# Moving VectorE and POOL instructions in the opening steps of a two-layer graph-attention kernel, and one block transpose in every later step

## Chip, cores and metric

One core of one Trainium2 chip. The metric is the device time of one execution in microseconds (us); the kernel before has a median of 3182.92 us over three executions (3182.58 to 3184.44). Engines are named as in the profile: PE is TensorE, DVE is VectorE, ACT is ScalarE, POOL is GpSimd, SP is SyncE.

## The reference, cut to what matters

64 graphs of 256 nodes with 512 features go through two layers of masked attention. Layer 0 has 4 heads of 64, layer 1 has 8.

```python
h = relu(layernorm(x));  x = x + L0(h, adj)      # layer 0
h = relu(layernorm(x));  x = x + L1(h, adj)      # layer 1
# L0:  q, k, v = h@Wq, h@Wk, h@Wv                (4 heads)
#      attn = softmax(where(adj, q k^T / 8, -max));  out = (attn v) @ Wo + bo
# L1:  h = layernorm(h)*gamma + beta;  q, k, v = split(h @ w_qkv^T)   (8 heads)
#      attn = softmax(where(adj | eye, q k^T / 8, -1e9)); out = (attn v) @ w_out^T + b_out
```

## The kernel before, in words

**Tiling.** The 64 graphs are done two at a time, so there are 32 steps (`s` = 0 to 31); a step's tokens are 512, in four row tiles of 128. Projections are done with seven products of half-size blocks in place of eight (`PRODUCT`, line 402). A **set** is those seven products of one matrix, on PE one after the other in the order 1, 6, 5, 2, 7, 3, 4 (`SET`). The sums of activations that products need are made by `act_sums0` and `act_sums1` on POOL (lines 412 to 417), the sums of weights by `weight_sum` (line 409).

**Banks.** Every product goes to one of four PSUM banks, taken in rotation by `mm_tile`. Products 1, 5 and 7 hold their bank, because 2, 3 and 4 accumulate in it later (`SHARED`). After a product a drain instruction has to read the bank: products 1 and 2 on ACT (lines 750 and 758), the others as an addition on DVE (lines 752 to 762, in the order 6, 5, 7, 3, 4). So product 3 can't begin before product 5 is drained, nor product 4 before product 7 is, and a later matmul that comes round to the same bank waits in the same way. Output projections (`combine`) drain the same way at lines 769 to 780.

**Softmax.** The pipeline calls attention work a **visit**: `scores` (PE, line 933), `mask_scores` (DVE, 956), `exponentials` (ACT, 961). The sums over keys go another way: `key_halves` adds the two key halves on POOL into the single buffer `pd` (968), `turn_keys` transposes `pd` in 32x32 blocks on DVE (974), `key_quarters` reduces that on DVE (981), and one visit later `key_sums` ends it on PE (1032), inverts it on DVE (1036) and sends it through DRAM to all partitions (`line`, 1043, then `oT<-line`, 1047). `weigh_out` multiplies by v (PE, 1004) and copies out on ACT (1016), `normalise` multiplies by the inverse on POOL (1063). A visit of layer 1, and of layer 0 after the first step, has two head pairs, i = 0 and 1; the first layer-0 step takes its two head pairs in visits of their own.

**Norms and transposes.** `norm0` makes the moments on DVE (589, 590) and, at the fourth tile, the scales on POOL; `scale_row` applies them on ACT (605). From step 2 on, the transpose of h in layer 0 goes by `turn_blocks` on DVE (699), `move_blocks`, 16 DMAs of SP (711), and `place_h` on ACT. `neighbours` (DVE, 524) finds rows with an edge and `neighbours_out` and `neighbours_in` send that through DRAM. `first_bias` (511) and `second_bias` (651) add the output biases to the residual tile `xt` on POOL; `load_graph` (505) loads `xt` from ACT's queue.

**What orders the work.** All of it is written out by hand: `at(period, place, fn, ...)` puts a call at time `6.4*period + place` (6.2 for negative periods), the list is sorted by that number, and the calls are made in that order (`for _, _, fn, args in sorted(events...)`). PE, DVE, ACT and POOL take their instructions strictly in that order (`manual_schedule` at line 359 names these four engines; SP is not among them). An engine that waits therefore holds back everything that comes later in its list. Within a period, step s has layer 1's first q/k set at 0, the output projection of the step before at 1, visit X at 2 (`AT_X`) with the v set of layer 1 from 2 to 3, layer 0's output projection of the next step at 3, layer 1's second q/k set at 3.5, the next visit at 4.5 (`AT_Q0`), and so on. Before step 0's period lie two opening periods, in which the weights are also transposed by PE (`weight_block`, 469, copied out at 474).

Of the kernel before, what the change touches and what calls it, by code (L numbers as in the profile page):

```python
# [315 lines left out]
def fast_path(  # L316
# [19 lines left out]
    nc = tc.nc  # L336
# [89 lines left out]
    wo1 = const.tile([P, NB, HP1, HD], FP, name="wo1")  # L426
# [261 lines left out]
    def by_tensor(s, lyr):  # L688

        return s == 0 or s == (1, NSTEP - 1)[lyr]  # L690
# [382 lines left out]
    def at(period, place, fn, *args):  # L1073
        events.append((period * (PERIOD if period >= 0 else FIRST) + place, len(events), fn, args))
# [15 lines left out]
    def visit(period, w, prev, cur):  # L1090

        w -= 0.0003
        s, lyr, prs = prev
        last = (s, lyr) == (NSTEP - 1, 1)
        if prs:
            if prs[0] == 0 and not last:
                at(period, w - 0.0002, place_values, s, lyr)
            at(period, w - 0.0001, key_sums, s, lyr, prs)
            for i, pr in enumerate(prs):
                if not last:  # L1100
                    at(period, w, weigh_out, s, lyr, pr)
                    at(period, w + (0.55 if len(prs) == 1 else (0.3, 0.75)[i]), normalise, s, lyr, pr)
        z, q = w > AT_Z - 0.01 and period < NSTEP - 2, abs(w - AT_Q0) < 0.01 and 0 <= period < NSTEP - 2
        for i, pr in enumerate(cur[2]):
            unit = (*cur[:2], pr)
            one = cur[:2] == (0, 0)
            at(period, w, scores, *unit, i == 1)
            at(period, w, mask_scores, *unit, 0)
            at(period, w + 1 / 7 if one else w, mask_scores, *unit, 1)
            for g, place in enumerate((0.05, 0.22) if one else ((0.02, 0.03), (0.15, 0.3))[i]):  # L1110
                at(period, w + place, exponentials, *unit, g)
            for e, place in enumerate((0.23, 0.3) if one else ((0.1, 0.11), (0.495, 0.496) if z else (0.435, 0.436) if q else (0.35, 0.36))[i]):
                at(period, w + place, key_halves, *unit, e)
            if cur[:2] == (1, 0):
                turn, add, key = 0.112, 0.113, (*cur[:2], (0, 1), pr)
            else:
                turn, add = (
                    (0.31, 0.311) if one else ((0.49, 0.491), (0.63, 0.92))[i] if z else
                    ((0.43, 0.431), (1.02, 1.021))[i] if q else ((0.29, 0.291), (0.6, 0.72))[i]
                )  # L1120
                key = (*cur, i)
            at(period, w + turn, turn_keys, cur[0])
            at(period, w + add, key_quarters, *key)

    AT_X, AT_C0, AT_QK, AT_Q0, AT_V0, AT_H1, AT_Z = 2.0, 3.0, 3.5, 4.5, 5.5, 6.06, 6.2
    LAST_QK = 4.0
    none, L0, L1A, L1B = (NSTEP, 0, ()), (0, 1), (0, 2), (1, 3)
    for s in range(NSTEP - 1):
        visit(s, AT_X, (s + 1, 0, L0), (s, 1, L1A))
        if s < NSTEP - 2:  # L1130
            visit(s, AT_Q0, (s, 1, L1A), (s, 1, L1B))
            visit(s, AT_Z, (s, 1, L1B), (s + 2, 0, L0))

    p = NSTEP - 2
# [15 lines left out]
    for s in range(NSTEP):  # L1150

        p = s - 2
# [5 lines left out]
        for t in range(NT):  # L1158
            at(p, (0.5 + 0.4 * t, 1.95 + 0.1395 * t)[s] if s < 2 else (0.95, 1.05, 1.2, 1.35)[t], norm0, s, t)
            if s == 0:  # L1160
                at(p, 0.95 + 0.4 * t, first_scale, t)
            else:
                at(p, 1.6 + 0.001 * t if s != 1 else 2.6 + 0.1 * t, scale_row, s, t)
            if not by_tensor(s, 0):
                at(p, AT_X - 0.00035 + 0.00001 * t, turn_blocks, s, 0, t)
        if not by_tensor(s, 0):
            at(p, AT_X - 0.00031, move_blocks, s)
        for g in range(G):
            at(p, (1.8, 2.7)[s] if s < 2 else 0.94 + 0.001 * g, neighbours, s, g)
        if s < 2:  # L1170
            at(p, (2.9, 2.72)[s], neighbours_rows, s)
            at(p, (FIRST_Q0 + 0.285, 3.59)[s], neighbours_turn, s)
        else:
            at(p, 0.945, neighbours_out, s)
            at(p, 1.9, neighbours_in, s)
        at(p, (FIRST_Q0 + 0.1425, 3.583)[s] if s < 2 else 2.5, adjacency_turn, s)
        at(p, (FIRST_Q0 + 0.3, 3.74)[s] if s < 2 else 3.1, mask0, s)
# [13 lines left out]
        for t in range(NT):  # L1191
            place = (FIRST_V0 + 0.14 * t - (0 if t else 0.0005), (4.31, 5.02, 5.16, 5.31)[t])[s] if s < 2 else AT_V0 + 0.14 * t
            at_dense(p, place, 0.14, project_v0, s, t)
        p = s - 1
        if s == 0:
            p -= 2.23 / FIRST
        edge = 0 if s == 0 else 1 if s == NSTEP - 1 else 2
        if edge < 2:
            at(p, (0.0, 0.2)[edge], load_x, s)
        else:  # L1200
            at(p, AT_X + 0.005, load_graph, s, 1)
            at(p, AT_X + 0.025, load_graph, s, 0)
        for k, t in enumerate(NORM1):
            at(p, (1.55, 1.5, (2.34, 2.5, 2.85, 2.86)[k])[edge], first_bias, s, t)
        if edge == 2:
# [9 lines left out]
        for k in range(NT):  # L1215
            at(p, ((2.901, 3.041, 3.181, 3.321), (2.99919, 2.99933, 2.99947, 2.99961), (3.79, 3.8, 3.94, 3.95))[edge][k], norm1, s, k)
            at(
                p, ((3.042, 3.182, 3.322, 3.323), (2.99948, 3.2, 3.3, 3.45), (4.08, 4.22, 4.23, 4.37))[edge][k],
                norm1_rest, s, k,
            )  # L1220
            at(p, (10.9 + 0.1 * k, 6.5 + 0.1 * k, 5.6 + 0.01 * k)[edge], second_bias, s, k)
            place = ((3.6112, 3.6113, 3.7502, 3.7503)[k], 3.6 + 0.01 * k, AT_Q0 - 0.0002 + 0.00001 * k)[edge]
            at(p, place, scale_row, s, NORM1[k])
            if edge == 2:
                at(p, AT_Q0 + (0.15, 0.16, 0.29, 0.3)[k], turn_blocks, s, 1, NORM1[k])
# [3 lines left out]
        turn = (3.763, 3.9995, AT_H1)[edge]  # L1229
# [4 lines left out]
        p = s  # L1234
        if s < NSTEP - 1:
# [3 lines left out]
            p, place = (s + 1, 1.0) if s < NSTEP - 2 else (s, LAST_QK + 2)  # L1239
# [5 lines left out]
        else:  # L1245
            p = s - 1
# [22 lines left out]
    for i in range(16):  # L1269

        place = (
            *(3.3 - 3.93 + (1 + k) / 7 - 0.0005 for k in range(7)), 0.5205,
            *(0.53 + 0.14 * (k + 1) - 0.0005 for k in range(4)), *(FIRST + 0.9995 for k in range(4)),
        )[i]
        at(-1, place, lambda i=i: weight_block(blocks[i // 4], i // 4, i % 4))
    for i in range(4):
        at(-1, 0.1 + 0.01 * i, weight_sum, nc.vector, wqkv1[:, :, :, 0, :], i)
        at(-1, 0.54 + 0.0001 * i, weight_sum, nc.gpsimd, wqkv1[:, :, :, 1, :], i)
        at(0, 0.3, weight_sum, nc.gpsimd, wqkv1[:, :, :, 2, :], i)
        at(0, 2.8 + 0.3 * i, weight_sum, nc.gpsimd, wo1, i)  # L1280
    for _, _, fn, args in sorted(events, key=lambda e: e[:2]):
        fn(*args)

# [1 line left out]
def kernel(tc, *args):  # L1285
    nc = tc.nc
    B, N, _ = args[0].shape
    P = 128
    with tc.tile_pool(name="guard", bufs=1) as guard:
        extremes = guard.tile([P, B // 2 * 3 + 4], FP, name="extremes")  # L1290
        ident = guard.tile([P, P], FP, name="ident")
        make_identity(nc, ident)
        fast_path(tc, *args, ident, extremes)
        safe = guard.tile([1, 1], I32, name="safe")
        with tc.tile_pool(name="gps", bufs=1, space=bass.MemoryType.PSUM) as ps:
            top = guard.tile([P, 1], FP, name="top")
            nc.vector.tensor_reduce(top, extremes, axis=mybir.AxisListType.X, op=ALU.max)
            row = ps.tile([1, P], FP, name="row")
            nc.tensor.transpose(row, top, ident)
            all_top = guard.tile([1, 1], FP, name="all_top")  # L1300
            nc.vector.tensor_reduce(all_top, row, axis=mybir.AxisListType.X, op=ALU.max)
            nc.vector.tensor_scalar(safe, all_top, LIMIT, None, op0=ALU.is_le)
        flag = nc.values_load(safe[0:1, 0:1], min_val=0, max_val=1, skip_runtime_bounds_check_because="a comparison gives 0 or 1")
        with tc.If(flag < 1):
            general_path(tc, *args)
# [29 lines left out]
```

## Time and profile before

| | before |
|---|---|
| median of three executions | 3182.92 us |
| the profiled execution, its own time | 3188.26 us |
| its span | 3186.3 us |
| PE busy | 3143.5 us, 99% |
| POOL busy | 2240.4 us, 70% |
| DVE busy | 2147.2 us, 67% |
| ACT busy | 1248.1 us, 39% |
| DMA engines, mean rate | 75 GB/s |
| granted PE clock, mean | 0.997 |

The profiled execution took 5.3 us more than the median; sums made from its rows are made against its own time. In the page, a row gives a line of the code, an engine, an operation, the count, busy time, the mean time of one in ns, and the idle time of that engine just before such instructions with what ended it. In a timeline, the first number is the start in us from the beginning of the span, the second the duration, and a bracket at the end is idle time before the piece and its releaser.

### The profile page before, as it was taken

To read this page: it belongs to the slowest core of one execution; us is meant where nothing else is said; L and a number is where in the kernel's file an instruction comes from. 1 tells how busy PE (TensorE), PEld (TensorE's weight loads), DVE (VectorE), ACT (ScalarE), POOL (GpSimd) and SP (SyncE) were. 2 spreads that over 40 slices of the span, in tenths; PEclk is the share of its full clock that TensorE was granted. 3 is DMA by queue.
4 is the path that set the end of the run, shared out by engine and by line. 5 is a ranking of instruction groups with operands and counts; after the bars stand their busy time and mean duration, and the time that the engine had idled before them with its cause. 6 is when DMAs were issued, how large, how long until landed. Compare 5 with 4: busy or idle time off the path is not lost.

```text
span 3186.3 us, 54549 instructions
## 1 busy us (share of the span) xinstructions
PE 3143.5 (99%) x20660; PEld 2584.4 (81%) x20660; DVE 2147.2 (67%) x3590; ACT 1248.1 (39%) x2226; POOL 2240.4 (70%) x2124
## 2 busy tenths in 40 slices
PE   8899999999999999999999999999999999999999
PEld 6688888888888888888888888888888888888887
DVE  6576676666766766766666666667666666666666
ACT  4343433444343434334343434343343434343431
POOL 6667767777667677677776676776777766767753
PEclk9999999999999999999999999999999999999999
DMA  3221322312223223223222232232231222322301
GB/s 125 65 81 53 90 64 80 90 54 81 72 79 85 81 54 90 65 80 92 56 77 72 79 85 76 59 90 64 81 92 56 76 72 79 85 69 64 91 28 48
DMA packets 179851, 237.42 MB, mean 75 GB/s; under 512 B 65272, under 2 KB 69504, under 8 KB 179584
## 3 DMA queue, kind: packets, MB, share of 16 engines
q1 hardware_dynamic: 162832, 202.02, 22.7%
q10 hardware_dynamic: 16752, 31.86, 3.2%
q8 instruction: 165, 2.70, 0.4%
q14 instruction: 102, 0.84, 0.1%
HBM read 136.45 MB, written 34.40 MB: 54 GB/s over the span
## 4 chain that ended last, share of the span: by engine, by line
PE 87%; POOL 6%; DMA 4%; DVE 1%; issue 1%; ACT 0%; SPq 0%; ACTq 0%; POOLq 0%; DVEq 0%
PE mm L816 36%; PE mm L873 16%; PE sc L1004 9%; PE mm L857 7%; PE sc L933 7%; PE mm L843 7%; PE mm L933 2%; DMA out_dram<-xt 2%; POOL xt L511 2%; POOL pd L968 2%; DMA xt<-in_x_dram 1%; POOL oT L1063 1%; PE mm L1032 1%; POOL xt L784 0%; PE mm L899 0%
## 5 line engine op out<-in xcount | busy, mean ns | idle before, releaser
L816 PE MATMUL mm<-hT,wqkv 128*128 128x256 f32 x3584 | 790.0, 381 | 5.4 <-DVE qk L754 5.4
L816 PEld LDWEIGHTS mm<-hT,wqkv 128*128 128x128 f32 x3584 | 679.0, 190 | 109.4 <-issue 11.8
L968 POOL TENSOR_TENSOR pd<-p 128x512 f32<-128x512 f32 x383 | 480.2, 1276 | 404.4 <-ACT p L961 266.5
L873 PE MATMUL mm<-wo,oT 128*128 128x256 f32 x2632 | 587.4, 381 | 7.4 <-POOL oT L415 5.2
L873 PEld LDWEIGHTS mm<-wo,oT 128*128 128x128 f32 x2632 | 498.5, 190 | 86.5 <-POOL n L573 8.0
L956 DVE TENSOR_TENSOR p<-sc,n 128x512 f32<-128x512 f32 x579 | 362.7, 681 | 266.8 <-PE sc L933 265.4
L961 ACT ACTIVATE p<-p 128x512 f32<-128x512 f32 x766 | 431.1, 623 | 135.7 <-DVE p L956 134.6
L857 PE MATMUL mm<-wqkv,hT 128*128 128x256 f32 x1792 | 404.9, 383 | 6.9 <-DVE v L756 6.8
L816 PE MATMUL mm<-hT,wqk 128*128 128x256 f32 x1792 | 400.3, 383 | 1.2 <-DVE qk L756 1.0
L857 PEld LDWEIGHTS mm<-wqkv,hT 128*128 128x128 f32 x1792 | 334.4, 190 | 64.5 <-DVE v L756 11.6
L816 PEld LDWEIGHTS mm<-hT,wqk 128*128 128x128 f32 x1792 | 339.0, 191 | 57.3 <-issue 11.7
L1004 PE MATMUL sc<-p,v 128*32 128x256 f32 x6128 | 351.5, 380 | 0.0
L784 POOL TENSOR_TENSOR xt<-xt,u 128x512 f32<-128x512 f32 x183 | 230.1, 1272 | 98.8 <-DVE xt L773 71.3
L933 PE MATMUL sc<-qk 64*128 64x256 f32 x2320 | 295.1, 386 | 3.4 <-ACT oT L1016 3.4
L974 DVE STREAM_TRANSPOSE turned_p<-pd 128x1024 f32<-128x1024 f32 x192 | 237.5, 1237 | 83.2 <-POOL pd L968 82.8
L1004 PEld LDWEIGHTS sc<-p,v 128*32 128x32 f32 x6128 | 190.2, 110 | 118.4 <-issue 0.3
L933 PEld LDWEIGHTS sc<-qk 64*128 64x128 f32 x2320 | 219.9, 187 | 62.9 <-issue 39.2
L1063 POOL TENSOR_TENSOR oT<-oT 128x512 f32<-128x512 f32 x188 | 240.3, 1278 | 4.9 <-DMA oT<-line 4.9
L605 ACT ACTIVATE h<-h,mr,r 128x512 f32<-128x512 f32 x252 | 184.8, 804 | 141.6 <-POOL mr L601 137.7
L981 DVE TENSOR_REDUCE part<-turned_p 128x32 f32<-128x1024 f32 x192 | 232.8, 1213 | 4.4
L843 PE MATMUL mm<-wv,hT 128*128 128x256 f32 x1024 | 227.0, 379 | 0.0
L843 PEld LDWEIGHTS mm<-wv,hT 128*128 128x128 f32 x1024 | 194.2, 190 | 26.8 <-issue 0.3
(141 smaller groups left out, 3743.2 us busy)
## 6 DMA issues: line engine op xcount, KB each, us to landing
h<-blocks SPq DMA_DIRECT2D x960, 64.0 KB, 2.0
oT<-line SPq DMA_DIRECT2D x376, 128.0 KB, 3.9
h<-in_x_dram SPq DMA_DIRECT2D x31, 1024.0 KB, 5.8
out_dram<-xt SPq DMA_DIRECT2D x62, 512.0 KB, 4.0
xt<-in_x_dram ACTq DMA_DIRECT2D x60, 512.0 KB, 6.6
ne<-row SPq DMA_DIRECT2D x30, 256.0 KB, 4.9
ad<-in_adj_dram SPq DMA_DIRECT2D x32, 128.0 KB, 8.9
wr<-in_L_gnn_w_qkv_dram SPq DMA_DIRECT2D x3, 1024.0 KB, 8.8
```

What stands on the lines that cost most here:

```text
L816: nc.tensor.matmul(bank[:, k, :], w[:, wa, c, k, a * P:(a + 1) * P], st["hT"][:, ba, c, :], start=first and (k, c) == (0, 0), stop=(k, c) ...
L843: nc.tensor.matmul(bank, st["hT"][:, b0 + t // NIC * step, c % HC, i:i + P], wv0[:, c, :], start=(c == 0), stop=(c == NC - 1),)
L857: nc.tensor.matmul(bank[:, t, :], st["hT"][:, ba, c, t * P:(t + 1) * P], wqkv1[:, wa, c, 2, :], start=first and (t, c) == (0, 0), stop=(t, ...
L873: nc.tensor.matmul(bank[:, t, :], oT[:, ba, c, t * P:(t + 1) * P], w[:, wa, c, :], start=first and (t, c) == (0, 0), stop=(t, c) == (NIC - ...
L933: nc.tensor.matmul(sc[g][e][:, kc, :], qk[rows, 1, k0:k0 + P], qk[rows, 0, g * N:(g + 1) * N], start=True, stop=True,)
L956: nc.vector.tensor_tensor(p[e][:, g], sc[e], neg[:, :, g, :], ALU.add)
L961: nc.scalar.activation(p[e][:, g], p[e][:, g], AF.Exp, scale=SCALE)
L968: nc.gpsimd.tensor_tensor(st["pd"][:, e], p[e][:, :, 0, :], p[e][:, :, 1, :], ALU.add)
L974: nc.vector.transpose(st["turned_p"], st.pop("pd").rearrange("p e g (b k) -> p (e g b) k", k=32))
L981: nc.vector.tensor_reduce(st["part", lyr, prs][:, i], st.pop("turned_p"), axis=mybir.AxisListType.X, op=ALU.add)
L1004: nc.tensor.matmul(po[r0:r0 + 32, g, :], st[f"v{lyr}"][:, g * NIC + kc, pr * P + r0:pr * P + r0 + 32], p[r0 // DH][:, g, kc, :], start=(kc ...
L1063: nc.gpsimd.tensor_tensor(dst, dst, invb, ALU.mult)
```

## The change

Only numbers in the hand-written order change, and with them the order of calls. No instruction is added or taken away.

- First layer-0 set, second head pair: `turn_keys` and `key_quarters` go from 0.31 to 0.53 of their visit, behind the copy of the first transposed weight block.
- Layer-0 visits of step 1: `turn_keys` and `key_quarters` of both head pairs, and `key_halves` of the second, go out of the opening into layer 1's first q/k set of step 0.
- Step 2: `neighbours` and `neighbours_out` go from 0.94 to 0.6; `scale_row` from 1.6 to 2.35; `turn_blocks` from just before visit X to 2.9 to 2.99, `move_blocks` to 3.0.
- Step 0: `second_bias` goes from 2.47 to 2.77 up to 0.95; the four weight sums of `wo1` go from 2.8 to 3.7 up to 1.1.
- Step 1: `load_graph` goes from 2.005 and 2.025 to 1.2.
- Visit X of every step (and the last visits): `turn_keys` of head pair i = 1 goes from 0.6 to 0.715, behind the drain of product 7 of v (0.7133); its `key_quarters` goes from 0.72 to 1.001 in visit X, behind the drain of product 4, and to 0.87 in the last visits.

```diff
             for e, place in enumerate((0.23, 0.3) if one else ((0.1, 0.11), (0.495, 0.496) if z else (0.435, 0.436) if q else (0.35, 0.36))[i]):
-                at(period, w + place, key_halves, *unit, e)
+                if unit == (1, 0, 1):
+                    at(0, 0.45 + place, key_halves, *unit, e)
+                else:
+                    at(period, w + place, key_halves, *unit, e)
             if cur[:2] == (1, 0):
-                turn, add, key = 0.112, 0.113, (*cur[:2], (0, 1), pr)
+                period, w, key = 0, 0.0, (*cur[:2], (0, 1), pr)
+                turn, add = ((0.44, 0.441), (0.715, 0.87))[pr]
             else:
                 turn, add = (
-                    (0.31, 0.311) if one else ((0.49, 0.491), (0.63, 0.92))[i] if z else
-                    ((0.43, 0.431), (1.02, 1.021))[i] if q else ((0.29, 0.291), (0.6, 0.72))[i]
+                    ((0.31, 0.311), (0.53, 0.531))[pr] if one else ((0.49, 0.491), (0.63, 0.92))[i] if z else
+                    ((0.43, 0.431), (1.02, 1.021))[i] if q else ((0.29, 0.291), (0.715, 1.001 if w < AT_X else 0.87))[i]
                 )
...
-                at(p, 1.6 + 0.001 * t if s != 1 else 2.6 + 0.1 * t, scale_row, s, t)
+                at(p, (2.6 + 0.1 * t, 2.35 + 0.001 * t)[s - 1] if s < 3 else 1.6 + 0.001 * t, scale_row, s, t)
             if not by_tensor(s, 0):
-                at(p, AT_X - 0.00035 + 0.00001 * t, turn_blocks, s, 0, t)
+                at(p, AT_X - 0.00035 + 0.00001 * t if s > 2 else 2.9 + 0.03 * t, turn_blocks, s, 0, t)
         if not by_tensor(s, 0):
-            at(p, AT_X - 0.00031, move_blocks, s)
+            at(p, AT_X - 0.00031 if s > 2 else 3.0, move_blocks, s)
         for g in range(G):
-            at(p, (1.8, 2.7)[s] if s < 2 else 0.94 + 0.001 * g, neighbours, s, g)
+            at(p, (1.8, 2.7)[s] if s < 2 else (0.6 if s == 2 else 0.94) + 0.001 * g, neighbours, s, g)
...
-            at(p, 0.945, neighbours_out, s)
+            at(p, 0.61 if s == 2 else 0.945, neighbours_out, s)
...
-            at(p, AT_X + 0.005, load_graph, s, 1)
-            at(p, AT_X + 0.025, load_graph, s, 0)
+            at(p, AT_X + 0.005 if s > 1 else 1.2, load_graph, s, 1)
+            at(p, AT_X + 0.025 if s > 1 else 1.2, load_graph, s, 0)
...
-            at(p, (10.9 + 0.1 * k, 6.5 + 0.1 * k, 5.6 + 0.01 * k)[edge], second_bias, s, k)
+            at(p, (9.38 + 0.001 * k, 6.5 + 0.1 * k, 5.6 + 0.01 * k)[edge], second_bias, s, k)
...
-        at(0, 2.8 + 0.3 * i, weight_sum, nc.gpsimd, wo1, i)
+        at(0, 1.1, weight_sum, nc.gpsimd, wo1, i)
```

## The prediction, made before the result was known

> **What bounds the kernel now.** I read the share of busy time first, then busy time by stretches of 100 us, then PE's own waits, then the timelines of PE, DVE and POOL around each wait. The stretches, with PE's busy time first, show where PE is not full.
>
> ```profile
> 0.00:100.00 100.00, 85.67 (x485) 66.63 (x485) 60.60 (x112) 44.25 (x88) 67.22 (x78) 0.98 0.38 120
> 100.00:200.00 100.00, 85.88 (x566) 68.16 (x567) 60.79 (x105) 36.36 (x67) 72.07 (x71) 0.93 0.22 61
> 200.00:300.00 100.00, 98.21 (x648) 80.91 (x647) 67.25 (x113) 39.58 (x71) 70.80 (x68) 1.00 0.27 75
> 900.00:1000.00 100.00, 99.99 (x657) 82.76 (x656) 68.59 (x116) 38.89 (x69) 71.30 (x68) 1.00 0.27 74
> ```
>
> PE is the bound: 99.99 of 100 us in the middle. What order alone can win lies in the first 160 us, with a few us later. PE's timeline names the places; the bracket is the idle time before the piece and what ended it.
>
> ```profile
> 52.44 0.66 PE L469 MATMUL mm<-ident,wr 128*128 128x128 f32 x4 [4.39 <-ACT wqkv L474]
> 103.99 5.61 PE L816 MATMUL mm<-hT,wqkv 128*128 128x256 f32 x16 [5.38 <-DVE qk L754]
> 120.23 1.40 PE L933 MATMUL sc<-qk 64*128 64x256 f32 x7 [3.41 <-ACT oT L1016]
> 137.50 1.99 PE L857 MATMUL mm<-wqkv,hT 128*128 128x256 f32 x8 [1.19 <-DVE v L756]
> 145.58 4.65 PE L873 MATMUL mm<-wo,oT 128*128 128x256 f32 x13 [5.22 <-POOL oT L415]
> 439.56 1.99 PE L857 MATMUL mm<-wqkv,hT 128*128 128x256 f32 x8 [0.58 <-DVE v L756]
> 446.90 1.10 PE L873 MATMUL mm<-wo,oT 128*128 128x256 f32 x4 [0.16 <-DVE xt L773]
> ```
>
> The five of the head sum to 19.6 us. Later, six waits for L756 (1.65, 0.58, 0.33, 0.51, 0.28, 2.21) make 5.6 us, and ten for L773 of about 0.16 make 1.6. The releaser of the second is a drain that stood behind two block transposes, and those behind POOL, as DVE's and POOL's timelines show:
>
> ```profile
> 96.13 1.25 DVE L974 STREAM_TRANSPOSE turned_p<-pd 128x1024 f32<-128x1024 f32 x1 [4.63 <-POOL pd L968]
> 100.04 1.25 DVE L974 STREAM_TRANSPOSE turned_p<-pd 128x1024 f32<-128x1024 f32 x1 [1.41 <-POOL pd L968]
> 103.24 0.69 DVE L754 TENSOR_TENSOR qk<-mm,qk 128x512 f32<-128x512 f32 x1
> 117.62 2.83 DVE L699 STREAM_TRANSPOSE blocks<-h 128x512 f32<-128x512 f32 x4 [2.18 <-issue]
> ```
>
> ```profile
> 99.97 5.30 POOL L409 TENSOR_TENSOR wqkv<-wqkv 128x512 f32<-128x512 f32 x4
> ```
>
> And SP's timeline, where the DRAM round of the key sums begins 3.6 us after the inverse is there (115.3 on DVE):
>
> ```profile
> 118.53 0.34 SPq L536 DMA_DIRECT2D ne<-row  x1
> 118.97 0.66 SPq L1043 DMA_DIRECT2D line<-inv  x1
> ```
>
> **What the Trainium skill says.** "TensorE: Matmul & The Clock Gate", section "What's actually happening", has PE's clock fall to half after an idle window of about 3.4 us. The trace agrees: after the wait of 5.38, 16 matmuls of L816 took 5.61 us where 40 at 89.71 took 8.90 (3.6 for 16), and the granted clock of 100 to 120 us is 0.83. So a long wait costs up to 2 us beyond itself. "GPSIMD Engine Reference", section "3.1 Elementwise", has a two-input addition about twice as long on POOL as on DVE; here 1276 against 681 ns (L968, L956), so POOL is the engine where order is dear. "DMA: Bandwidth & Descriptors", section "Issuing engines are not separate DMA queues", says transfers of all queues share the 16 engines; here `line` took 6.33 us beside a 512 KB load of ACT's queue, against a median of 2.5.
>
> **The change, part by part.** Times are on the clock of the profile before. Product lengths: 8 matmuls 1.76 us (12.28 for 56, L816), 4 of L873 0.88; drains on DVE 0.68.
>
> *First set.* Transpose and reduction (1.25 + 1.22) now stand behind the weight-block copy, but still ahead of the drain of product 6. The next weight block starts at 48.1 and ends at 48.6; product 5 then takes product 6's bank (three rotate, one is held). DVE: POOL's `pd` is unchanged, transpose 49.15, reduction to 51.6, drain to 52.25. PE waits 3.7 us there. Product 5 began at 52.93; now 52.3. Gain 0.6, not 4.4.
>
> *Step 1's key sums into step 0's set.* Product 5's drain comes before the transpose now: 5.38 is gone. But POOL does the four sums of wqkv1 (place 0.3) before the second `key_halves` (place 0.55): 96.1 + 5.3 + cast 1.04 + 2.5 = 104.95. DVE: first transpose and reduction to 98.6, `neighbours` 1.27 to 99.9, drain of product 7 to 100.6, so product 4 waits 0.2 behind product 3 (ends 100.4) and ends at 102.4. Two weight blocks (0.45 each) go on to 103.3. The third needs product 3's bank, whose drain is behind the second transpose (104.95 to 106.2): 106.9, a wait of 3.6. The fourth needs product 4's drain, behind the reduction (108.1) and one `norm0` (0.87): 109.6, a wait of 2.1. So 5.9 of new waits take the place of 5.6, but key sums start at 110.3 in place of 111.86, since the clock is full and DVE's reductions were moved.
>
> *Step 2's scaling and block transposes out of visit X.* Four transposes (2.83) leave DVE, four scalings (3.0) leave ACT, which made PE wait 3.41. What covers is v's set: DVE has 2.9 us of idle time there before L974 at 135.62. PE's path from key sums to the v set is then as in a later step (2757.22 to 2764.70, 7.5 us), with DVE's inversion late by three `norm0` (to 114.2) but masks not needed before 115.3: v starts at 118.0 (before: 125.18). `move_blocks`: SP's 16 issues take 11.07 and the last lands 2 later; from 133.8 that is 147, and `place_h` is due at about 150. Slack 3 us, cost nothing.
>
> *POOL's biases and weight sums earlier, loads earlier.* After 104.95 POOL does wo0's sums 3.14, second biases 5.0, wo1's sums 5.06, step 2's scales 1.9: 120.1. `key_halves` of visit X: 122.6. `line` goes out at 114.3 without waiting for SP's `ne<-row` (118.53 before), and lands in 2.5 to 6.3, I take 4.4: 118.7; issue of two copies 1.2, landing 4.5 (chain of waits): 124.4. Then normalise 1.27, bias 1.27, halves 2.5, bias 1.27, normalise 1.27, sums 0.73 and 0.74: 133.45. The v set (12.3) and the output product 1 (0.9) end at 131.3 now that L756's 1.19 is gone, so product 6 waits 2.1 in place of 5.22. Two more sums and two biases (4.0) put the addition of product 2 at 137.4; with two drains, product 4 starts at 138.9 and ends at 139.8. Low clock after the 3.6 wait: bounded by 0 and 2, I take 1. First set's gain, -0.6. The next set starts at 140.2; before, 152.7. **Gain 12.5 us.** Pure POOL work from 93.6 to that sum is 38 us, so 131.6 even without a wait of POOL: the gain can't pass 15 or so by this path.
>
> *Visit X in every step.* At 439.56 the drain of product 7 stood behind a transpose that waited for POOL; now it doesn't. But POOL runs from 430.22 to 445.43 without a pause, its last bias there releases product 2's addition, and product 4 starts at 446.90 whatever product 4 of v did. All six waits lie in such steps, so I put their 5.6 us at **nothing**; bounds -5.6 and, since the reduction of 1.2 us now precedes the drain of the output's product 6, which has 1.10 + 0.16 us of idle DVE ahead of it (930.48, 931.33 in a full step), +0.1 a step, 3. The last visits have no waits of PE: nothing.
>
> Sum: 3188.26 - 12.5 = 3175.8 for the profiled execution; 3182.92 - 12.5 = **3170.4** for the median, the 5.3 us between them kept.
>
> **Rivals.** *All head waits vanish*: 19.6 + 0.2, about 4 of low clock: -24, 3159. For it, each has its releaser moved. Against it, the `pd` of POOL still comes ahead of drains at 51.6 and 106.2. *POOL takes back more*: `line` lands late beside the 1 MB that `load_graph` now moves, as at 118.97, and the output's product 6 waits 5 as before; with late `key_halves` about 6 us less gain, 3176. For it: POOL's chain is already the tighter one. *More steps are POOL-bound*: steps of the middle take 97.16, bound ones 97.4 to 99.8, an excess of 8.5 us in all; if all 29 lose 0.65 it is 19, or 10 more, 3180.5. *Slower: SP puts the moved block copies late.* SP's order isn't written by hand: the adjacency of step 2 went at 40.48, ahead of h at 87.93, behind which the code has it. If the 16 copies go behind the next visit's `line` and its four copies (issue at about 154, then 4.4), the last lands at 171.5 in place of 147, `place_h` ends at 174 ahead of `weigh_out` in ACT's list, and scores stop from 158 on: 16.5 and 3.4 of low clock. -12.5 + 19.9 = +7.4: 3190. It decides from copies that land after about 163; for it speaks only that freedom.
>
> **How the numbers follow.** Forecast 0.62 (3166 to 3175.5), all vanish 0.09, POOL takes back 0.15, more bound steps 0.08, SP late 0.06. A measurement of this kernel can tell about 0.2% (6.4 us) from no change. Faster by more: 0.62 + 0.09 + 0.6 of 0.15, 0.80. Slower: 0.05. Within: 0.15. The range takes in the forecast, most of POOL's case, and the unknown landing and clock (3 us either way): 3163.5 to 3179.
>
> **What would show it.** PE's waits: about 3.7 near 52, two near 103 to 110 for L760 and L762 before the weight blocks, none for L1016, about 2 for L415 near 131; L756 gone from PE's waits but L773's still there and longer in the same steps. The second q/k set of step 0 starts near 140. Wrong if the waits at 103 are missing (POOL's order then isn't what I take it for), or if step lengths in the middle change.

## The result, and the profile after

The changed kernel takes 3167.07 us (median of five executions, 3166.64 to 3168.69), the kernel before in the same series 3182.58: 15.5 us less, a ratio of 0.9953 with a 95% interval of 0.9939 to 0.9968. The forecast was 3170.4, 12.5 us less.

The two profiled executions differ by more: spans of 3186.3 and 3164.9, 21.4 us. The profiled execution before stood 5 us above its median and the one after did not, so their difference is not the gain. Behind the start of the second q/k set of step 0 the two traces take 3033.7 and 3027.1; e2 below, which has visit X as it was, takes 3026.2 there, so the place of that transpose doesn't explain the difference. The stretches of the changed kernel's trace (PE's busy time first after the length) show the second hundred at 94.63 in place of 85.88.

```profile
0.00:100.00 100.00, 87.56 (x497) 68.63 (x498) 63.66 (x117) 44.15 (x88) 69.66 (x80) 0.98 0.37 120
100.00:200.00 100.00, 94.63 (x626) 76.44 (x625) 69.15 (x119) 40.25 (x73) 82.34 (x78) 0.97 0.22 64
```

PE's timeline of the changed kernel has these waits left in the places of the forecast; the last two lines stand for two kinds of later wait.

```profile
51.54 3.64 PE L816 MATMUL mm<-hT,wqk 128*128 128x256 f32 x8 [3.71 <-DVE qk L752]
99.16 1.97 PE L816 MATMUL mm<-hT,wqkv 128*128 128x256 f32 x8 [0.21 <-DVE qk L756]
105.33 0.66 PE L469 MATMUL mm<-ident,wr 128*128 128x128 f32 x4 [3.33 <-DVE qk L760]
107.84 1.12 PE L469 MATMUL mm<-ident,wr 128*128 128x128 f32 x4 [1.86 <-DVE qk L762]
109.24 5.46 PE L1004 MATMUL sc<-p,v 128*32 128x256 f32 x64
136.78 1.10 PE L873 MATMUL mm<-wo,oT 128*128 128x256 f32 x4 [0.16 <-DVE xt L773]
429.86 1.10 PE L873 MATMUL mm<-wo,oT 128*128 128x256 f32 x4 [0.18 <-DVE xt L773]
3089.79 0.27 PE L1032 MATMUL mm<-quarters,part 128*64 128x32 f32 x2 [0.28 <-DVE part L981]
```

No wait for L1016 and none for L415 is left. The wait for L760 is read from DVE's and POOL's timelines: the drain stands behind a transpose, that waited 4.43 us for POOL's `pd`, and POOL did the weight sums first.

```profile
103.45 1.25 DVE L974 STREAM_TRANSPOSE turned_p<-pd 128x1024 f32<-128x1024 f32 x1 [4.43 <-POOL pd L968]
104.62 0.65 DVE L760 TENSOR_TENSOR qk<-mm,qk 128x512 f32<-128x512 f32 x1
```

```profile
94.66 5.32 POOL L409 TENSOR_TENSOR wqkv<-wqkv 128x512 f32<-128x512 f32 x4
100.93 2.48 POOL L968 TENSOR_TENSOR pd<-p 128x512 f32<-128x512 f32 x2
118.58 2.50 POOL L968 TENSOR_TENSOR pd<-p 128x512 f32<-128x512 f32 x2
121.04 1.27 POOL L1063 TENSOR_TENSOR oT<-oT 128x512 f32<-128x512 f32 x1
129.81 0.73 POOL L415 TENSOR_TENSOR oT<-oT 128x256 f32<-128x256 f32 x1
```

From 92 to 134 us POOL is busy for 40.35 of 42 us (22.95 in the same stretch before). The second q/k set of step 0 begins at 137.72, before at 152.69. That is 15.0 us, of which 0.8 had arisen by the first set (its wait for L756 ended at 25.75 against 26.51, and no edit lies ahead of that). The opening is worth **14.2 us**.

### The profile page after: what moved, and what is told of

Same layout as the page of the kernel before. It is cut to its first block, busy times and chain, and to the rows that moved or that the text cites. A ratio compares the mean times of both kernels' runs of the same rounds, so it can differ in the third digit from the quotient of the medians.

```text
span 3164.9 us, 54517 instructions
## 1 busy us (share of the span) xinstructions
PE 3136.4 (99%) x20660; PEld 2582.6 (82%) x20660; DVE 2145.3 (68%) x3590; ACT 1248.7 (39%) x2226; POOL 2237.7 (71%) x2124
## 4 chain that ended last, share of the span: by engine, by line
PE 91%; POOL 3%; DMA 2%; DVE 2%; issue 1%; ACT 0%; SPq 0%; ACTq 0%; POOLq 0%; DVEq 0%
PE mm L816 36%; PE mm L873 17%; PE sc L1004 10%; PE mm L857 10%; PE sc L933 8%; PE mm L843 7%; PE mm L933 2%; DMA out_dram<-xt 1%; POOL xt L511 1%; POOL pd L968 1%; DMA xt<-in_x_dram 1%; PE mm L1032 1%; PE mm L899 0%; POOL oT L1063 0%; DMA h<-in_x_dram 0%
## 5 line engine op out<-in xcount | busy, mean ns | idle before, releaser
L1004 PE MATMUL sc<-p,v 128*32 128x256 f32 x6128 | 353.3, 382 | 0.0
L1004 PEld LDWEIGHTS sc<-p,v 128*32 128x32 f32 x6128 | 190.7, 110 | 119.7 <-issue 2.3
```

Of the source, the lines that this page charges most:

```text
L1004: nc.tensor.matmul(po[r0:r0 + 32, g, :], st[f"v{lyr}"][:, g * NIC + kc, pr * P + r0:pr * P + r0 + 32], p[r0 // DH][:, g, kc, :], start=(kc ...
```

## The experiments

Each median is compared with runs of the kernel before taken beside it. e8 to e10 ran on a chip where that kernel took 3199 us, e11 and e12 on one with 3188; there only the ratios are read.

| run | median | before beside it | ratio, 95% interval |
|---|---|---|---|
| e1, visit X's transpose alone | 3181.44 | 3180.31 | 1.0004, 0.9996 to 1.0012 |
| e2, all but that | 3166.56 | 3180.31 | 0.9955, 0.9942 to 0.9969 |
| e3, change + v's sums behind halves | 3166.00 | 3180.31 | 0.9955, 0.9942 to 0.9969 |
| e4, change + first transpose later | 3163.20 | 3180.31 | 0.9945, 0.9931 to 0.9958 |
| e5, change + POOL relieved | 3167.01 | 3180.47 | 0.9956, 0.9943 to 0.9970 |
| e6, e5 + e3 | 3163.75 | 3180.47 | 0.9949, 0.9936 to 0.9963 |
| e7, e6 + e4 + normalise later | 3158.41 | 3180.47 | 0.9929, 0.9916 to 0.9943 |
| e8, step 1's key sums alone | 3191.76 | 3199.08 | 0.9978, 0.9971 to 0.9985 |
| e9, step 2's blocks alone | 3198.02 | 3199.08 | 0.9995, 0.9986 to 1.0004 |
| e10, POOL and loads alone | 3191.61 | 3199.08 | 0.9978, 0.9971 to 0.9986 |
| e11, e7 + last visits as before | 3164.24 | 3188.48 | 0.9919, 0.9905 to 0.9932 |
| e12, the kernel before again | 3187.99 | 3188.48 | 1.0000, 0.9993 to 1.0007 |

**e1 and e2: is the transpose of visit X worth its waits?** The theory was that POOL sets those steps, the rival that the waits for L756 are lost time.

```diff
# e1: the only edit to the kernel before. e2: the changed kernel with this line as it was.
-                    ((0.43, 0.431), (1.02, 1.021))[i] if q else ((0.29, 0.291), (0.6, 0.72))[i]
+                    ((0.43, 0.431), (1.02, 1.021))[i] if q else ((0.29, 0.291), (0.715, 1.001 if w < AT_X else 0.87))[i]
```

> The kernel before with one edit: in visit X the second block transpose goes behind the drain of product 7 of v, its reduction behind product 4. Theory (POOL sets those steps): PE's waits for L756 vanish, but those for L773 in the same steps grow, and in step 0 the wait of 5.22 for L415 grows by about 1.2. Time within 1 us of before (3182.6), perhaps 0.8 more for three waits of 0.28 at the last visits. Rival (the transpose's place was the cost): the 1.2 of step 0 and most of the 5.6 us of the middle are gained, 3176 to 3178.

> The changed kernel with the second block transpose of visit X (and of the last visits) put back to its old place. Theory: POOL sets the steps where this matters, so the time stays within 1.5 us of the changed kernel (3167.1), and the waits of 0.28 at the last visits go (0.8 less). Rival: 4 to 6 us of the gain came from this edit, 3171 to 3173.

e1 is 1.1 us above the runs beside it (interval -1.3 to 3.8), e2 has the changed kernel's ratio within 0.0002. PE's timeline of e1 shows where the time stayed: no wait for L756 is left, L415's has grown from 5.22 to 5.99, and the wait for L773 in the early steps has grown.

```profile
143.73 6.25 PE L873 MATMUL mm<-wo,oT 128*128 128x256 f32 x20 [5.99 <-POOL oT L415]
443.49 1.10 PE L873 MATMUL mm<-wo,oT 128*128 128x256 f32 x4 [0.64 <-DVE xt L773]
```

On that chip the rival's 4 to 6 us are out. In step 0 most of the removed wait was paid again a few microseconds later: of the 1.19 for L756, the wait for L415 took back 0.77, and a new one for L773 took 0.16. For the middle of the program the two runs show less than that. The trace of e2, with the transpose at its old place, has only two waits for L756 between 200 and 3000 us, of 0.18 and of 0.70, so in such an execution there was little to win:

```profile
2075.46 1.99 PE L857 MATMUL mm<-wqkv,hT 128*128 128x256 f32 x8 [0.70 <-DVE v L756]
```

The traces of e8 to e10, from the chip of 3199 us, have 9.5 to 11.7 us of these waits. What the edit is worth there was not tried.

**e3: what are the two waits before the weight blocks worth?**

```diff
-        at(0, 0.3, weight_sum, nc.gpsimd, wqkv1[:, :, :, 2, :], i)
+        at(0, 0.57, weight_sum, nc.gpsimd, wqkv1[:, :, :, 2, :], i)
```

> The changed kernel with the four weight sums of wqkv1's v part put behind the second key_halves of step 1 on POOL (place 0.57 for 0.3), so that POOL does the halves 5.3 us earlier. Theory A (the two waits of 3.33 and 1.86 us before the weight blocks cost what they show, with 1.8 of low clock behind them): the first goes, the second falls to about 1.3, key sums start 4.6 us earlier at full clock: 6 us less, about 3161. Theory B (POOL is full from 92 to 131 us, so that its sums for the output product come at the same time whatever PE does before): the waits at the weight blocks go but product 6 of step 1's output projection then waits about 5 us for L415, and the time stays within 1.5 us of 3167.1.

Theory B held: the same ratio as e2, 0.9955. Its traces say where the time went. PE's waits, then the DVE piece behind them:

```profile
104.45 0.66 PE L469 MATMUL mm<-ident,wr 128*128 128x128 f32 x4 [0.88 <-DVE qk L762]
126.02 5.27 PE L857 MATMUL mm<-wqkv,hT 128*128 128x256 f32 x16 [3.27 <-DVE v L754]
136.93 1.10 PE L873 MATMUL mm<-wo,oT 128*128 128x256 f32 x4 [0.16 <-DVE xt L773]
```

```profile
122.78 1.25 DVE L974 STREAM_TRANSPOSE turned_p<-pd 128x1024 f32<-128x1024 f32 x1 [4.92 <-POOL pd L968]
```

The wait of 3.33 is gone and that of 1.86 is 0.88, but visit X's `pd` still leaves POOL at 122.7 and PE waits 3.27 there. The place of the new wait was not the one expected (L754 in the v set, not L415 after it); the cause was, POOL's full queue. The last piece of the output projection starts at 136.93, against 136.78.

Another bound stood close behind. On DVE the inverse begins 3.7 us earlier than in the changed kernel (108.04 against 111.74), but SP sends `line` behind `ne<-row`, and the copies of `line` go out later than in the changed kernel. The first three lines are the changed kernel's, the other three e3's:

```profile
106.77 0.34 SPq L536 DMA_DIRECT2D ne<-row  x1
112.10 0.47 SPq L1043 DMA_DIRECT2D line<-inv  x1
115.71 2.37 SPq L1047 DMA_DIRECT2D oT<-line  x4
109.89 0.34 SPq L536 DMA_DIRECT2D ne<-row  x1
110.28 0.60 SPq L1043 DMA_DIRECT2D line<-inv  x1
116.49 2.38 SPq L1047 DMA_DIRECT2D oT<-line  x4
```

**e4: the first set.** Its transpose goes behind product 6's drain, where the change had put it behind the weight-block copy only.

```diff
-                    ((0.31, 0.311), (0.53, 0.531))[pr] if one else ...
+                    ((0.31, 0.311), (0.656, 0.657))[pr] if one else ...
```

> The changed kernel with the transpose and reduction of the first set's second head pair put behind the drain of product 6 (place 0.656 for 0.53), just ahead of its key sums. Theory: the wait of 3.71 us for L752 goes, a wait of about 0.9 for L981 before the key sums takes its place, and the low clock after it goes: 4.4 us less at the key sums, 3163. Rival: something else sets the opening soon after (a transfer or POOL), and less than 1 us of it is left at the end, 3166 to 3167.

The wait of 3.71 is replaced by this one, at the key sums:

```profile
52.50 0.19 PE L1032 MATMUL mm<-quarters,part 128*32 128x32 f32 x1 [1.13 <-DVE part L981]
```

In its trace the last product of step 1's output projection starts at 133.79, 3.0 earlier than in the changed kernel although its opening ran 1.4 late (27.20 against 25.75 at the first wait for L756). The medians taken beside each other give 2.8 to 3.4 (against e3 and e2), less than the 4.4 expected. The mechanism is as expected; the size in the median is uncertain by a few us, since its five executions (3160.8 to 3166.3) overlap with those of e2 and e3.

**e5, e6 and e7: what lies behind POOL.**

```diff
# e5
-        at(0, 1.1, weight_sum, nc.gpsimd, wo1, i)
+        at(0, 3.56, weight_sum, nc.gpsimd, wo1, i)
-            at(p, (9.38 + 0.001 * k, ...)[edge], second_bias, s, k)
+            at(p, (12.01 + 0.001 * k, ...)[edge], second_bias, s, k)
# e6: this and e3's edit. e7: those, e4's edit and
-                    at(period, w + (... (0.3, 0.75)[i]), normalise, s, lyr, pr)
+                    at(period, w + (... (0.37 if (s, lyr) == (1, 0) else 0.3, 0.75)[i]), normalise, s, lyr, pr)
```

> The changed kernel with 10.3 us of POOL's work (wo1's four weight sums and step 0's second biases) put behind step 1's output projection, to 3.56 and 3.58. POOL is full from 92 to 134 us in the changed kernel, but PE waits for it there only through the two waits before the weight blocks (3.33 and 1.86), which lie ahead of the moved work, and 0.16 later. Theory (several bounds lie on top of each other): no gain alone, within 1 us of the changed kernel. Rival (POOL's fullness as such costs time): 3 us less or more.

> The same, and the weight sums of v's part behind the second key_halves as well (the edit that gained nothing alone). POOL is then free by about 118 us. Theory A (POOL was the only bound): the wait of 3.27 for L754 goes and nothing takes its place, 5 to 6 us less than the changed kernel. Theory B (behind POOL lies the DRAM round of the key sums: line issued at 110.3, landed at 116.5, its copies landed at about 121): normalise starts at 121.5 at the earliest, its chain of 8.7 us ends at 130, and product 6 of the output projection waits about 3 us for L415: 1 to 2.5 us less than the changed kernel.

> All that helped or should: POOL's relief, the sums behind the halves, the first set's transpose behind product 6, and step 1's first normalise put behind the key halves of visit X (0.37 for 0.3), so that POOL does 3.8 us of other work while the DRAM round is under way. If theory B is right, normalise's chain then ends at about 127, the wait for L415 is under 0.5, and the gains add: 4 (first set) and 5 (step 0), 9 less than the changed kernel, 3157 to 3159. If another bound follows, 5 to 6 less.

e5 gains nothing and e3 gains nothing, but both together gain 3.3 us against e5 (four of the five executions of e6 lie below all of e5's, the fifth among them). Neither theory of e6 had the size: POOL and PE in its trace show the DRAM round as the next bound, with a smaller wait than theory B's 3.

```profile
118.86 1.28 POOL L1063 TENSOR_TENSOR oT<-oT 128x512 f32<-128x512 f32 x1 [4.42 <-DMA oT<-line]
```

```profile
127.81 4.58 PE L873 MATMUL mm<-wo,oT 128*128 128x256 f32 x20 [1.57 <-POOL oT L415]
```

The copies had landed at 118.86, not at 121.5. Here too `line` went out behind `ne<-row`, at 109.38, though the inverse was ready at 107.44, and its copies went out 5.9 us after it. No run moved `ne<-row` out of the way, so what that order costs is open. In e7 POOL works under the round, L415's wait is gone, and the gains add up: 8.6 us below e5, as expected. Its PE clock shows no low stretch in the opening at all (10.2 us of one in the changed kernel, 17.1 before), and these are the largest waits after 90 us there:

```profile
99.92 0.66 PE L469 MATMUL mm<-ident,wr 128*128 128x128 f32 x4 [0.88 <-DVE qk L762]
127.69 1.10 PE L873 MATMUL mm<-wo,oT 128*128 128x256 f32 x4 [0.46 <-DVE xt L773]
```

e7 beats both kernels: its five executions (3156.3 to 3159.3) lie below all five of e5 in the same series (3165.9 to 3167.2), and e5 is as fast as the changed kernel.

**e8, e9 and e10: the parts alone.** e8 holds the edits of `key_halves`, `turn_keys` and `key_quarters` of step 1 and of `neighbours`; e9 those of `scale_row`, `turn_blocks` and `move_blocks`; e10 those of `load_graph`, `second_bias` and wo1's sums, each as in the diff above.

> The kernel before with one part: step 1's key sums moved into step 0's first set, and step 2's neighbours earlier. Theory: the wait of 5.38 goes, waits of about 3.5 and 2 before the weight blocks come, line no longer waits behind the row transfer: 2 to 4 us less than before. The waits for L1016 (3.41) and L415 (3 to 5) stay.

> The kernel before with one part: step 2's scaling, block transposes and their 16 copies out of visit X. Theory: the wait of 3.41 for L1016 goes and v starts 5 us earlier, but POOL's chain to L415 hangs on the DRAM round and the second biases in between, so product 6 of the output projection waits some 5 us longer: within 1.5 us of before. Rival (the wait is worth what it shows): 5 us less.

> The kernel before with one part: second biases and wo1's sums earlier on POOL, step 1's loads earlier. Theory: the wait of 5.22 for L415 goes, but the 10.3 us now lie ahead of step 2's row scales, which ACT's scaling and so the copies L1016 wait for: that wait grows from 3.41 to about 8; in all 3 to 5 us less than before. Rival: the whole 5.2 and its low clock, 6 to 7 less.

The waits of PE that the comparison rests on: e8, one line; then e9, two; then e10:

```profile
141.28 8.48 PE L873 MATMUL mm<-wo,oT 128*128 128x256 f32 x24 [4.57 <-POOL oT L415]
```

```profile
137.31 3.78 PE L857 MATMUL mm<-wqkv,hT 128*128 128x256 f32 x8 [4.25 <-DVE v L756]
145.40 4.97 PE L873 MATMUL mm<-wo,oT 128*128 128x256 f32 x14 [2.93 <-POOL oT L415]
```

```profile
124.81 2.13 PE L933 MATMUL sc<-qk 64*128 64x256 f32 x7 [8.37 <-ACT oT L1016]
```

In e8 the waits before the weight blocks came as expected (3.32 and 1.86), and the one for L1016, which was to stay at 3.41, fell to 1.21. e9's removal of four transposes from visit X bought nothing that can be measured: 1.6 us by the ratio (0.9995 of 3182.6), the interval reaching past zero. Its theory had the cause but not the places. POOL's first normalise waits for the DRAM round until 130.47, against 130.63 before, so the sum that releases L415's wait starts at 144.60, against 144.79. But the wait for L1016 fell to 2.27 only, and what PE won came back in the v set, at L756 (4.25 for 1.19), while L415's wait grew smaller (2.93 for 5.22). e10 made the wait for L1016 8.37, as computed, and removed L415's. The sizes of e8 and e10 were too small in the expectation: both gain about 7 us (0.9978; 4.5 to 9.3 by their intervals) where 2 to 4 and 3 to 5 were written, and e10 fell to its rival's number while showing the theory's waits. In their traces the second q/k set of step 0 begins at 149.59 and 149.77, about 3 us ahead of the 152.69 in the trace of the kernel before, which is the size expected, but 5.5 ahead of the 155.13 in e12, which is that kernel on the chip of 3188 us and has 27.3 us of half clock in its opening (17.1 in the first trace of it, and in e8 and e10). No trace of the kernel before was taken on their own chip, so where the other 3 to 4 us lie is open. The three add to 15.6 us, about the whole, so these runs don't show that the parts hinder each other, only that the middle one alone is worth little.

**e11 and e12.**

```diff
# e11, e7 with
-                    ... ((0.29, 0.291), (0.715, 1.001 if w < AT_X else 0.87))[i]
+                    ... ((0.29, 0.291), (0.715, 1.001) if w < AT_X else (0.6, 0.72))[i]
# e12: the kernel before, unchanged
```

> The combined kernel with the second block transpose and its reduction of the three last visits back at 0.6 and 0.72. Theory: the three waits of 0.28 for L981 before the key sums of the last visits go and no other wait comes, 0.8 us less than the combined kernel (3158.4, a ratio of 0.9929 to before), so a ratio of about 0.9926. Rival: a drain of a q/k product stands behind a transpose again, as in the middle visits, and PE waits there for as much or more.

> The kernel before, unchanged, for a second trace. Theory (the waits of the middle, L756 and L773, hang on when loads and stores land, and differ from execution to execution): the waits of the opening stay within 0.3 us each (4.4, 5.4, 3.4, 1.2, 5.2), but those between 200 and 3000 us come in other steps and their sum of 7.2 us changes by over 1.5. Rival (they belong to certain steps of the order): the same steps, the same sum within 1 us.

In e11 the three waits of 0.28 are gone and no other came in the last visits; that 0.8 us can't be told in the median (0.9919 against 0.9929, with overlapping intervals). e12 decides less than hoped. The waits between 200 and 3000 us sum to 8.3 against 7.2, a change between the theory's 1.5 and the rival's 1, in mostly the same early and late steps (343, 441, 637, 1709, 1807, 2781 us again) with other sizes and some new ones. So the order of work seems to say which steps are near the edge, and the execution, or the chip, how far over. In the opening, L756's wait was 2.15 and L415's 3.53 (1.19 and 5.22 before), against the expectation: most of what the v set loses, the output projection gives back (5.7 us for the two, 6.4 before).

## Why the prediction was right

Step by step of its sum; the opening's offset of 0.8 is taken out of the times after.

- *First set, 0.6 and a wait of 3.7.* Measured 3.71; product 5 began 1.39 earlier, 0.63 without the offset. Right, and e4 shows that the rest of that wait was the place of the drain.
- *Step 1's key sums: new waits of 0.2, 3.6 and 2.1.* Measured 0.21, 3.33 and 1.86; key sums at 109.65 (108.89 in the trace) where 110.3 less 0.6 was forecast. Right to the mechanism.
- *Low clock 1, between 0 and 2.* The 64 matmuls of L1004 took 5.46 us after these waits, 3.66 in later steps, and the last weight block 1.12 where the one ahead of it took 0.66: 1.8 and 0.5, above the bound. The sum has a slip here too: it adds the 1 at the end of a chain that POOL sets, in which PE waits 2.1 us for POOL. A PE that comes 1 later would have waited 1.1 instead. Without the slip the forecast's own terms give a gain of 13.5.
- *Output projection: product 6 waits 2.1.* No wait. This is the term that was off, from both sides. `line` went out 0.8 earlier than forecast and landed in 3.6 us where 4.4 was taken, and POOL found the copies there at 121.04 after working without a pause, so its chain ended at 130.54. The forecast had put that at 133.45 (132.1 with its own 0.6 and the offset), 1.5 us late. And PE, slowed by the low clock, came to product 6 at 131.8 only. DVE rather than POOL then ended the set: it worked without a pause from 127.72 to 137.35, the four block transposes among it, and PE's wait of 0.16 for L773 stands behind that.
- *Visit X in every step: nothing.* Right for the time in e1 and e2, on a chip where e2 shows 0.9 us of these waits and not 5.6. The trace of the changed kernel shows the signature, L756 gone and L773 left.
- *Last visits: nothing.* Wrong by 0.8: three key sums wait 0.28 each for a reduction put at 0.87. e11 takes them away.
- *Block transposes and copies: slack 3.* The copies made no wait of PE, but there was a cost on ACT that the forecast missed: the copies read the buffer that step 1's `h` takes next, so its first scaling waited 2.05 us for them.

```profile
145.23 0.72 ACT L647 ACTIVATE h<-xt,mv 128x512 f32<-128x512 f32 x1 [2.05 <-DMA h<-blocks]
```

So the opening gave 14.2 in place of 12.5. At the start of the v set it stood 0.6 us behind the forecast (119.0 with the offset, where 118.0 + 1 - 0.6 was written), behind the output projection 1.7 ahead of it: 2.4 more from that stage, 1.0 of which is the slip. 14.2 less 0.8 is 13.4 of the 15.5; the last 2.1 lie in the middle of the program or in scatter (the five executions before spread over 3.6 us), and no run here tells which. The mechanism of the opening was right, but the nearness of the number is partly luck: a clock cost that was too small, a chain of POOL put too late and a cost counted twice nearly cancel. Of the rivals, none came: the order of SP in particular left the 16 copies at 132.57, right behind their transposes.

## What to carry to other kernels

When every engine takes work in a fixed order, price a wait by what releases the *next* one: here removing 4.3 us of waits (e3) or the 1.19 of step 0 (e1) paid nothing that could be measured, since POOL's queue or a DRAM round came due a few microseconds later at nearly the same time as before. Look for the wait on the chip and in the execution whose time you compare: those of the middle were 0.9 us in one trace and 11.7 in another. Add up the pure work of the suspected engine between two of its releases; where it fills the gap, only moving work out of that stretch and mending the order together pays (e3 0, e5 0, both 3.3). And count buffer reuse and the low clock after a wait among the costs of a moved step.

## What the runs showed of the hardware that was not expected

Half clock came in stretches of 3.41, 6.83 or 10.24 us in the opening of every trace that had any, and the same wait did not always bring the same stretch. The wait of 3.7 us ahead of product 5 was followed by 3.41 in the changed kernel, e2, e5 and e6, and by 6.83 in e3. The pair of waits of 3.3 and 1.9 us with 0.7 us of work between them brought 6.83 each time (changed kernel, e2, e5, e8). In e12 a wait of 2.15 us ended at 138.49 and half clock ran from 139.08 to 142.49; waits of 2.27 in e9 and e10 brought none.

How soon the 8 KB write `line` of step 0's visit X let its copies go went with SP's order and not with the loads beside it. In nine traces SP had issued `ne<-row` about 0.4 us ahead of `line`, and the copies went out 5.7 to 8.1 us after `line` (6.3 before, 6.2 in e3). In the other five `ne<-row` was 4.8 us or more ahead, and it took 1.7 to 3.6 us; in four of these, the changed kernel among them, 1 MB of loads had been issued less than 3 us before. No run moved that transfer alone, so its being the cause is not shown.
